# A second tap of VectorE's 3x3 convolution made by ScalarE and added by an accumulating DMA, with the later parts of that convolution one slot later

## The chip, the cores and the metric

The kernel runs on one core of a Trainium2 chip. The metric is device time in microseconds. Three runs of the kernel before took 6636.07, 6640.18 and 6641.82 us (median 6640.18). One more execution was taken with a profile.

## The reference, cut to what matters

The input is x of shape (8, 32, 128, 128), float32: eight images of 32 channels. For the normalised image, block matching picks for each pixel the 8 best of 25 shifts, and the shifted copies are stacked to 256 channels (xb). Then three pairs of a 1x1 convolution and a depthwise 3x3 convolution follow:

```
h = relu(conv(conv(xb, w1), w2, groups=CK, pad=1))
h = relu(conv(conv(h, w3), w4, groups=CK, pad=1))
wiener = sigmoid(conv(conv(h, w5), w6, groups=CK, pad=1))
filt = conv(wiener * dct, inv_dct_w, groups=C)
return conv(filt, agg_w)          # added to x; then a norm and a 5x5 convolution
```

A depthwise 3x3 convolution is, for each channel, a sum of nine shifted copies ("taps") of its image, each multiplied by a weight. All sums are in float32.

## The kernel before, in words

An image is cut into strips of eight rows; a step handles one strip, and there are 17 steps for each of the eight images, 136 in all. Each step has four slots, in the order i = 3, 2, 1, 0. Slot i = 1, 2 or 3 runs convolution pair i ("stage i") on a strip that is older the higher i is; slot 0 multiplies by the dct (`final_dct`, L795 on) and later sums up (`final_add`, L819 on). The strip that stage i began in its slot is read by stage i+1 in the next step, three slots later, and stage 3's by slot 0 of the same step, also three slots later.

The 256 channels are two halves of 128. One half's 3x3 convolution runs on TensorE (`pointwise_t`, `depthwise_t`: matmuls of L694 into p, copy to t at L701, shifted copies t<-t by DMA, matmuls of L750 into pw, activation at L763). The other half's runs on VectorE (`pointwise_v`, `depthwise_v`): the 1x1 result pv (L670) is copied by ScalarE to tv (L678); ScalarE makes the first tap into acc (L721); VectorE adds eight more with scalar_tensor_tensor (L724), in place; ScalarE applies relu or sigmoid (L728); a DMA moves the last two rows of tv to its top for the next strip (`rows_before_v`, L655).

`depthwise_v` is a generator, and the loop over the slots calls its parts. For a stage that begins in slot k: the ScalarE tap is written in slot k, the eight VectorE taps later in slot k, the activation in slot k+1, the row copy in slot k+2. The variables `new_v`, `dv` and `kept` hold the generators of this slot, the last one and the one before that. Slot 0 begins no stage, so it has an empty generator. Inside a slot the order is:

```
pointwise_v; first tap (ScalarE)       # pv, tv, L721
next(later); run("P"); final_dct       # pa (slot 3) ; L809, L817 (slot 0)
run("Q"); gather_select (0,)           # pd ; sel on ScalarE
gather_load; tick(b, i)                # ib ; other work on VectorE
next(later); next(new_v)               # xr, L838 ; VectorE taps, L724
pointwise_t; next(kept)                # p, t ; L655
gather_pixels; next(dt); run("A")      # pg, xb L638 ; pw L750 ; squares L452
next(dv); gather_select (1,); next(dt) # L728 ; sel ; L763
```

The order on TensorE, VectorE and ScalarE is this program order (`manual_schedule`). TensorE, VectorE, ScalarE, POOL (GpSimd) and SP (SyncE) each work their own instructions one after the other; POOL's and SP's are nearly all DMA issues.

Three other things go on beside the stages. The gather: matmuls pg (L631) on selection masks (sel, two ScalarE instructions each, L616 and L617), copied to xb (L638). The block matching of the next image: differences on VectorE (df, L444), squares on ScalarE (L452), matmuls pd (L459), then costs, maxima and places. And the last layer of the image before. Their work is handed out by `tick`, which gives VectorE 0.4 of a step's share in slot 0 and 0.2 in each of slots 3, 2 and 1. Once per image, `sources` writes the next image in another layout (xl, L411, then 32 transfers xtd<-xl in a row, L424 and L429, all from POOL's queue).

PSUM results of many kinds share five buffers in turn (pool `ps_x`): among them pv, p, pg, pa and pc. Each acc tile has one buffer per stage and half.

Of the kernel before, what the change touches and what calls it, by code (L numbers as in the profile page):

```python
# [8 lines left out]
F32 = mybir.dt.float32  # L9
# [3 lines left out]
AF = mybir.ActivationFunctionType  # L13
ALU = mybir.AluOpType
ORDERED = {mybir.EngineType.PE, mybir.EngineType.DVE, mybir.EngineType.Activation}

P = 128
C, K, H, W = 32, 8, 128, 128
CK = C * K
NO = 25  # L20
R = 8
# [23 lines left out]
def bm3d_conv_preact(  # L45
# [16 lines left out]
    nc = tc.nc  # L62
# [60 lines left out]
    dwv = const.tile([P, 3, 9], F32, name="dwv")  # L123
    for n, w in enumerate((w2, w4, w6)):
# [22 lines left out]
        op0=ALU.mult,  # L147
        op1=ALU.add,
# [38 lines left out]
    accp = ctx.enter_context(tc.tile_pool(name="acc", bufs=1))  # L187
# [23 lines left out]
    def push(task):  # L211
        want = next(task, None)
        if want:
            which, cost, *wait = want
            queues[which].append((cost, task, now[0] + (wait[0] if wait else 0)))
# [132 lines left out]
    def bands():  # L348

        nc.sync.dma_start(kb, k5.rearrange("a b -> (a b)").partition_broadcast(P))  # L350
        for dx in range(5):
            yield "D", 1.8
            nc.vector.tensor_scalar(
                band[:, dx], cst[:, 0:P], kb[:, dx : dx + 1], None, op0=ALU.mult
            )
            for i in range(1, 5):
                nc.vector.scalar_tensor_tensor(
                    band[:, dx],
                    cst[:, i : i + P],
                    kb[:, 5 * i + dx : 5 * i + dx + 1],  # L360
                    band[:, dx],
                    op0=ALU.mult,
                    op1=ALU.add,
                )

    def prep(b):

        xn = load_image(b, nc.gpsimd) if b else first
        yield "P", 0
        yield "D", 5.5  # L370
        st = work.tile([P, 8, 6], F32, name=f"st_{b}", tag="st")
        for i in range(8):
            nc.vector.bn_stats(
                st[:, i], xn[:, 3 + 4 * i : 7 + 4 * i, 2 : 2 + W]
            )
        mv = work.tile([P, 2], F32, name=f"mv_{b}", tag="mv")
        nc.vector.bn_aggr(mv, st.rearrange("p a b -> p (a b)"))
        yield "A", 0
        nc.scalar.copy(xn[:, :, 0:2], xn[:, :, 2:3].to_broadcast([P, HR, 2]))
        nc.scalar.copy(  # L380
            xn[:, :, 2 + W :], xn[:, :, 1 + W : 2 + W].to_broadcast([P, HR, 2])
        )
        mr = yield from group_stats(mv, f"a{b}")
        nc.vector.tensor_scalar(
            xn, xn, mr[:, 0:1], mr[:, 1:2], op0=ALU.subtract, op1=ALU.mult
        )
        push(sources(b, xn))

        idx = work.tile([P, 4, 8, K, 4], U32, name=f"idx_{b}", tag="idx", bufs=1)

        sq = dram.tile([NO // 2, 4, HR - 2, HX], F32, name=f"sq_{b}", tag="sq")
        for i in range((HR - 2) // SR):
            pd = ps_d.tile([P, SR // 2, HX], F32, name=f"pd_{b}_{i}", tag="pd")

            for aa in ((2, 4), (0, 0), (1, 1), (3, 2), (4, 3), (5, 5)):
                yield "D", PAIR
                push(squares(b, i, pd, xn, aa, sq, idx))
# [254 lines left out]
    def rows_before_v(i, b, n):  # L652
        v = tv[i - 1]
        if n < NS:
            nc.sync.dma_start(v[:, 0:2], v[:, R : R + 2])  # L655
        else:
            nc.gpsimd.memset(v[:, 0 : i + 1], 0.0)
# [52 lines left out]
    def depthwise_v(i, b, n):  # L710
        v = tv[i - 1]
        nr = R if n < NS else i
        out_ = accp.tile([P, R, W], F32, name=f"acc{i}_{b}_{n}_1", tag=f"acc{i}1")
        acc = out_[:, :nr]
        for k, (dy, dx) in enumerate(
            ((1, 1), (0, 0), (0, 1), (0, 2), (1, 0), (1, 2), (2, 0), (2, 1), (2, 2))
        ):
            tap = dwv[:, i - 1, 3 * dy + dx : 3 * dy + dx + 1]
            rows = v[:, dy : dy + nr, dx : dx + W]
            if k == 0:  # L720
                nc.scalar.activation(acc, rows, AF.Copy, scale=tap)  # L721
                yield out_
            else:
                nc.vector.scalar_tensor_tensor(  # L724
                    acc, rows, tap, acc, op0=ALU.mult, op1=ALU.add
                )
        yield
        nc.scalar.activation(acc, acc, funcs[i - 1])  # L728
        yield
        rows_before_v(i, b, n)  # L730
# [266 lines left out]
    def unit(stage, u, *rest):  # L997
        if 0 <= u < len(units) and units[u]:
            if stage is gather_load:
                at = (units[u][0], units[u][1] % 8 // 2)  # L1000
                until(lambda: at in ready, 4.0)
            stage(*units[u], *rest)
# [20 lines left out]
    def turn(credit):  # L1023
        now[0] += 1
        run("D", credit)
        run("A")
        run("P")
        run("Q")

    def until(cond, credit):  # L1030
        while not cond():
            turn(credit)

    with tc.manual_schedule(engines=ORDERED):
        push(prep(0))
        push(weights())
        push(mixes())
        xbd[0] = dram.tile([P, 2, H, W], F32, name="xbd_0", tag="xbd")
        for i in range(3):
            nc.gpsimd.memset(tb[i][0:64, :, 0], 0.0)  # L1040
        for u in range(7):
            unit(gather_load, u)

            for _ in range({2: 3, 3: 1}.get(u, 0)):
                turn(4.0)
            unit(gather_select, u - 2)
            unit(gather_pixels, u - 3)
        u = 4

        dt = dv = kept = iter(())  # L1050

        later = iter(())

        for s in range(len(steps) + 2):
            if s < len(steps):
                b, n = steps[s]
                if s == 2:
                    push(bands())
                if n == (0 if b else 4) and b + 1 < NB:
                    until(lambda: b in ready, 4.0)  # L1060
                    push(prep(b + 1))
                if n == NS - 1 and b + 1 < NB:
                    until(lambda: b + 1 in ready, 4.0)
                    xbd[b + 1] = dram.tile([P, 2, H, W], F32, name=f"xbd_{b+1}", tag="xbd")
            for i in (3, 2, 1, 0):
                si = s - (i - 1 if i else 2)
                live = 0 <= si < len(steps)
                new_v = new_t = iter(())
                if live:
                    bi, ni = steps[si]  # L1070

                if live and i:
                    src = source(i, bi, ni)
                    pointwise_v(i, bi, ni, lws[i - 1], src)
                    new_v, new_t = depthwise_v(i, bi, ni), depthwise_t(i, bi, ni)
                    accs[i, bi, ni] = [None, next(new_v)]
                next(later, None)
                if live and not i:
                    if ni == 0:
                        x1d[bi] = dram.tile([C, H, W], F32, name=f"x1d_{bi}", tag="x1d")  # L1080
                        stats[bi] = work.tile([P, NS + 1, 6], F32, name=f"stat_{bi}", tag="stat")
                    xr, xf, j0, j1 = fins.pop(si)
                run("P")
                if live and not i:
                    final_dct(bi, ni, accs[3, bi, ni], xf, j0, j1)

                run("Q")
                if s < len(steps):
                    unit(gather_select, u + 1, (0,))
                    unit(gather_load, u + 3)  # L1090
                    tick(b, i)
                next(later, None)
                next(new_v, None)
                if live and i:
                    pointwise_t(i, bi, ni, lws[i - 1], src)
                next(kept, None)
                if s < len(steps):
                    unit(gather_pixels, u)
                next(dt, None)
                run("A")  # L1100
                next(dv, None)
                if s < len(steps):
                    unit(gather_select, u + 1, (1,))
                    u += 1
                next(dt, None)
                kept, dv, dt = dv, new_v, new_t
                if live and not i:
                    later = end(bi, ni, xr, j0, j1)
                if not i and 0 <= s - 1 < len(steps):
                    fins[s - 1] = final_load(*steps[s - 1])  # L1110
        next(kept, None)
        for _ in later:
            pass
        until(lambda: {(NB - 1, 0), (NB - 1, 1)} <= done, 4.0)
# [62 lines left out]
```

## Time and profile before

| | |
|---|---|
| profiled execution, its own time | 6645.45 us |
| its span, first to last instruction | 6643.7 us |
| median of three runs | 6640.18 us |
| mean granted TensorE clock | 0.978 |
| TensorE busy | 6238.3 us, 94% |
| VectorE busy | 5862.9 us, 88% |
| ScalarE busy | 5054.4 us, 76% |
| POOL busy | 3079.3 us, 46% |
| data moved by DMA | 886.20 MB |

Busy is time with an instruction at work; the rest of the span an engine waits. A line of a group reads: line, engine, operation, result<-inputs, shape, xcount, then busy time in us, mean ns of one, and the idle time before them with what ended it. A line of the waits reads: engine, its tile and line, "<-" what it waited for, then total us, times, longest us. PE is TensorE, DVE is VectorE, ACT is ScalarE. A timeline line reads: start us, duration us, engine, line, operation, result<-inputs, shape, xcount. A line of the DMA issues ends with the size of one in KB and the median us from issue to landing.

### The profile page before, as it was taken

What the parts mean: (1) busy time and instruction counts of PE and PEld (TensorE: products, weight loads), DVE (VectorE), ACT (ScalarE), POOL (GpSimd) and SP (SyncE); (2) the same over time, 40 slices, a digit from 0 to 9 for tenths busy, and PEclk for the clock granted to TensorE, in tenths of its full rate; (3) what the DMA queues carried; (4) which work ended last, traced back from release to release, by engine and by line L of the source; (5) the groups of instructions that cost most, each with busy time, mean ns of one, the idle gap of its engine ahead of it and who ended that gap; (6) DMA issues with size and microseconds to landing.
All of it is one profiled execution on the core that took longest, in us unless ns stands there. A gap on an engine that the chain in (4) does not pass through costs nothing.

```text
span 6643.7 us, 234197 instructions
## 1 busy us (share of the span) xinstructions
PE 6238.3 (94%) x102306; PEld 3236.5 (49%) x102306; DVE 5862.9 (88%) x8828; ACT 5054.4 (76%) x6698; POOL 3079.3 (46%) x5015
## 2 busy tenths in 40 slices
PE   5898899999999999999999999999999999999997
PEld 1444455544555545544555544554445544454553
DVE  7889988999889998898989998899888999887786
ACT  5787778777787777877778877887769777687772
POOL 8354346444464343643446444464435543344334
PEclk8899999999999999999999999999999999999998
DMA  4555555656555564655646656465555655556553
GB/s 85 126 138 130 131 131 130 148 134 140 131 143 136 130 147 118 149 134 133 144 121 147 147 126 149 120 154 136 130 137 132 148 136 130 125 141 145 137 133 82
DMA packets 770751, 886.20 MB, mean 133 GB/s; under 512 B 248880, under 2 KB 614000, under 8 KB 769728
## 3 DMA queue, kind: packets, MB, share of 16 engines
q0 software_dynamic: 383648, 611.87, 36.9%
q1 hardware_dynamic: 383568, 258.11, 17.6%
q8 instruction: 805, 13.19, 0.9%
q10 hardware_dynamic: 2512, 1.25, 0.1%
q14 instruction: 218, 1.79, 0.1%
HBM read 420.60 MB, written 216.49 MB: 96 GB/s over the span
## 4 chain that ended last, share of the span: by engine, by line
PE 43%; DVE 29%; DMA 9%; ACT 8%; POOL 6%; issue 4%; SPq 0%; ACTq 0%; DVEq 0%; POOLq 0%
DVE acc L724 20%; PE pw L750 14%; PE pv L670 11%; PE p L694 9%; PE pg L631 3%; DMA t<-t 3%; POOL xtd L424 2%; DVE df L444 2%; DVE idx L537 2%; PE pc L809 2%; ACT sel L616 2%; ACT df L452 2%; DMA xf<-xbd 2%; DVE acc L817 1%; PE p L923 1%
## 5 line engine op out<-in xcount | busy, mean ns | idle before, releaser
L724 DVE SCALAR_TENSOR_TENSOR acc<-tv,dwv,acc 128x1024 f32<-128x1024 f32 (+3 forms) x3264 | 4032.3, 1237 | 240.8 <-ACT acc L721 136.8
L750 PE MATMUL pw<-t,dwd 96*32 96x254 f32 (+7 forms) x31680 | 2124.6, 420 | 51.0 <-DMA t<-t 38.4
L750 PEld LDWEIGHTS pw<-t,dwd 96*32 96x32 f32 (+1 forms) x31680 | 1088.4, 110 | 874.5 <-issue 411.2
L616 ACT ACTIVATE sel<-ib,nplace 128x1024 f32<-128x1024 uint8 x1024 | 1172.1, 1145 | 37.4 <-DMA ib<-idxd 37.4
L617 ACT ACTIVATE sel<-sel 128x1024 f32<-128x1024 f32 x1024 | 1085.7, 1060 | 32.5
L694 PE MATMUL p<-acc,lw 128*32 128x256 f32 x16768 | 1002.9, 383 | 24.7 <-ACT tv L678 23.3
L670 PE MATMUL pv<-acc,lw 128*32 128x512 f32 x8448 | 956.2, 590 | 48.7 <-DVE acc L817 43.4
L602 POOL DMA_DIRECT2D ib<-idxd x512 | 292.5, 571 | 1241.8 <-ACT sel L616 1176.2
L790 POOL DMA_DIRECT2D xf<-xbd x1088 | 651.9, 631 | 316.1 <-PE pc L809 180.1
L694 PEld LDWEIGHTS p<-acc,lw 128*32 128x32 f32 x16768 | 579.2, 111 | 437.1 <-issue 79.4
L452 ACT ACTIVATE df<-df 128x786 f32<-128x786 f32 (+2 forms) x576 | 468.6, 861 | 340.5 <-DVE df L444 337.8
L631 PE MATMUL pg<-sel,xt 120*32 120x88 f32 (+1 forms) x24576 | 616.1, 244 | 63.6 <-ACT sel L617 50.7
L631 PEld LDWEIGHTS pg<-sel,xt 120*32 120x32 f32 x24576 | 556.8, 110 | 235.0 <-ACT sel L617 70.1
L678 ACT COPY tv<-pv 128x512 f32<-128x512 f32 (+2 forms) x784 | 437.1, 579 | 305.0 <-PE pv L670 293.0
L444 DVE TENSOR_TENSOR df<-xn 128x786 f32<-128x786 f32 (+2 forms) x576 | 531.6, 973 | 81.2 <-PE pd L459 80.2
L728 ACT ACTIVATE acc<-acc 128x1024 f32<-128x1024 f32 (+3 forms) x408 | 417.3, 1023 | 241.6 <-DVE acc L724 241.3
L763 ACT ACTIVATE acc<-pw 128x512 f32<-128x512 f32 (+2 forms) x808 | 438.5, 573 | 182.7 <-PE pw L750 182.0
L670 PEld LDWEIGHTS pv<-acc,lw 128*32 128x32 f32 x8448 | 286.0, 111 | 534.1 <-issue 428.7
L701 ACT COPY t<-p 128x512 f32<-128x512 f32 x800 | 424.4, 571 | 118.0 <-PE p L694 118.0
L721 ACT ACTIVATE acc<-tv,dwv 128x1024 f32<-128x1024 f32 (+3 forms) x408 | 454.9, 1115 | 33.9 <-PE pa L830 20.6
L670 PE MATMUL pv<-xb,lw 128*32 128x512 f32 x4096 | 473.5, 596 | 0.0
L694 PE MATMUL p<-xb,lw 128*32 128x256 f32 x8192 | 468.5, 379 | 1.0 <-DVE xy L935 0.9
(155 smaller groups left out, 5932.9 us busy)
## 6 DMA issues: line engine op xcount, KB each, us to landing
ib<-idxd POOLq DMA_DIRECT2D x512, 256.0 KB, 4.1
xbd<-xb POOLq DMA_DIRECT2D x128, 1024.0 KB, 5.9
xf<-xbd POOLq DMA_DIRECT2D x960, 128.0 KB, 7.1
t<-t SPq DMA_DIRECT2D x792, 128.0 KB
t<-t SPq DMA_DIRECT2D x384, 256.0 KB
tv<-tv SPq DMA_DIRECT2D x384, 130.0 KB
xt<-xtd POOLq DMA_DIRECT2D x240, 180.0 KB, 3.7
xtd<-xl POOLq DMA_DIRECT2D x192, 96.0 KB, 3.5
```

What stands on the lines that cost most here:

```text
L444: nc.vector.tensor_sub(df[:, :, ca:cz], xn[:, r0 : r0 + SR, ca:cz], xn[:, r0 + dy : r0 + dy + SR, ca + dx : cz + dx],)
L452: nc.scalar.activation(df[:, :, ca:cz], df[:, :, ca:cz], AF.Square)
L616: nc.scalar.activation(sel, ib, AF.Square, bias=nplace)
L617: nc.scalar.activation(sel, sel, AF.Relu, scale=-1.0, bias=1.0)
L631: nc.tensor.matmul(pg[C * j : C * (j + 1), :, :, xa:xz], xt[: 8 * QW, f * (NT // 2) + t], sels[j // 2][: 8 * QW, j % 2 * 2 : j % 2 * 2 + 2 ...
L670: nc.tensor.matmul(ps[C * j : C * (j + 1), :hr], lhsT[:, g, P + C * j : P + C * (j + 1)], src(g)[:, h : h + hr], start=g == 0, stop=g == 1,)
L694: nc.tensor.matmul(ps[C * r : C * (r + 1), e, :nb], lhsT[:, g, s], rows[:, r : r + 4 * nb - 3 : 4], start=g == 0, stop=g == 1,)
L721: nc.scalar.activation(acc, rows, AF.Copy, scale=tap)
L724: nc.vector.scalar_tensor_tensor(acc, rows, tap, acc, op0=ALU.mult, op1=ALU.add)
L750: nc.tensor.matmul(pt[u][C * j : C * (j + 1), ka:kz, :nb, xa:xz], dwd[0:hi, i - 1, u, j, dx + 1], t[0:hi, j, ka:kz, :nb, xa + dx : xz + dx ...
L763: nc.scalar.activation(rows[:, u : u + 2 * nh[u] - 1 : 2, :nb], pt[u][:, : nh[u], :nb], funcs[i - 1])
L790: nc.gpsimd.dma_start(xf[p : p + C, m, j0:j1], src[g, m, (h + m + 1) % 2, :, :, ya:yz])
```

## The change

In `depthwise_v` ScalarE makes two taps: (1, 1) into acc as before, and (0, 0) into a new tile "more" with one buffer. A DMA from POOL's queue adds "more" to acc (`accum_op=ALU.add`). VectorE adds the other seven taps. The taps of VectorE now come after the first yield, and the loop calls them in slot k+1, the activation in slot k+2 and the row copy in slot k+3; `dv1`, `dv2` and `dv3` hold the generators of the last three slots. The places inside a slot where taps, activation and row copy are called stay the same, and so does `tick`.

```
+        more = accp.tile([P, R, W], F32, name=f"more{i}_{b}_{n}", tag="more")[:, :nr]
         acc = out_[:, :nr]
-        for k, (dy, dx) in enumerate(
-            ((1, 1), (0, 0), (0, 1), (0, 2), (1, 0), (1, 2), (2, 0), (2, 1), (2, 2))
-        ):
-            tap = dwv[:, i - 1, 3 * dy + dx : 3 * dy + dx + 1]
+        def tap(dy, dx):
             rows = v[:, dy : dy + nr, dx : dx + W]
-            if k == 0:
-                nc.scalar.activation(acc, rows, AF.Copy, scale=tap)
-                yield out_
-            else:
-                nc.vector.scalar_tensor_tensor(
-                    acc, rows, tap, acc, op0=ALU.mult, op1=ALU.add
-                )
+            return rows, dwv[:, i - 1, 3 * dy + dx : 3 * dy + dx + 1]
+        for to, at in ((acc, (1, 1)), (more, (0, 0))):
+            rows, scale = tap(*at)
+            nc.scalar.activation(to, rows, AF.Copy, scale=scale)
+        nc.gpsimd.dma_start(acc, more, accum_op=ALU.add)
+        yield out_
+        for at in ((0, 1), (0, 2), (1, 0), (1, 2), (2, 0), (2, 1), (2, 2)):
+            rows, scale = tap(*at)
+            nc.vector.scalar_tensor_tensor(
+                acc, rows, scale, acc, op0=ALU.mult, op1=ALU.add
+            )
         yield
         nc.scalar.activation(acc, acc, funcs[i - 1])
...
-                next(new_v, None)
+                next(dv1, None)
...
-                next(kept, None)
+                next(dv3, None)
...
-                next(dv, None)
+                next(dv2, None)
...
-                kept, dv, dt = dv, new_v, new_t
+                dv3, dv2, dv1, dt = dv2, dv1, new_v, new_t
```

## The prediction

> **What bounds the kernel now.** I read the page's busy shares first, then TensorE's waits, then the three engines' timelines around one boundary between slots. The page:
>
> ```profile
> PE 6238.3 (94%) x102306; PEld 3236.5 (49%) x102306; DVE 5862.9 (88%) x8828; ACT 5054.4 (76%) x6698; POOL 3079.3 (46%) x5015
> ...
> PE 43%; DVE 29%; DMA 9%; ACT 8%; POOL 6%; issue 4%; SPq 0%; ACTq 0%; DVEq 0%; POOLq 0%
> ...
> L724 DVE SCALAR_TENSOR_TENSOR acc<-tv,dwv,acc 128x1024 f32<-128x1024 f32 (+3 forms) x3264 | 4032.3, 1237 | 240.8 <-ACT acc L721 136.8
> ```
>
> The 94% is real work: 96 matmuls of L750 take 5.3 us wherever I look, in crowded stretches and in quiet ones, so nothing is stretched. The view by windows gives PE 5941 us busy in the 6200 us between 200 and 6400. Its idle time there is 259 us, 1.9 us for each of the 136 steps (8 images x 17). That is all that relief on another engine can give back. TensorE's waits (total us, times, longest) say who could:
>
> ```profile
> PE pi L569 <- DVE oc L560: 63.2, 16, 20.2
> PE pg L631 <- ACT sel L617: 50.7, 33, 2.3
> PE pd L459 <- ACT df L452: 46.6, 47, 3.6
> PE pv L670 <- DVE acc L817: 43.4, 25, 3.0
> PE pw L750 <- DMA t<-t: 38.4, 27, 4.0
> ```
>
> The first, third and fourth come from a late VectorE (df is made there). VectorE's 29% of the chain is mostly where it runs beside a TensorE that is busy anyway. So the change relieves the second engine, and what matters is whether it adds a wait to the first.
>
> **What goes and comes.** 408 taps leave VectorE: 408 x 1.237 = 505 us (5863 to 5358). 408 taps come to ScalarE: the present L721 tap takes 1.115 us in the mean, so +455 us (5054 to 5509). 408 accumulating transfers, up to 512 KB each, come to POOL's queue: at 0.5 to 0.8 us an issue (rows xf 0.63, xl 0.76) 200 to 330 us more of POOL's 46%.
>
> **What moves.** Taps, activation and row copy of the VectorE half each run one slot later than now. A step has slots 3, 2, 1, 0; stage i+1 consumes stage i three slots after it began. Now the activation L728 lies in the second slot, a whole slot ahead of its reader. After the change it lies at the end of the third, and the reader opens the next slot. What stands between them, stage by stage:
> - Stage 3: L728 at the end of slot 1; its reader is VectorE's L817 in slot 0. TensorE's pw (5.3) and pc (1.9) lie between: free.
> - Stage 2: L728 in slot 0; pw (5.3 us) lies between it and stage 3's pv. ScalarE needs the xb copy 0.6, perhaps squares 1.7, L728 1.06: covered.
> - Stage 1: L728 falls in slot 3, which has no pw, as slot 0 begins no stage. TensorE goes from pg straight to stage 2's pv (slot 2). Nothing lies between.
>
> TensorE and then ScalarE at that last boundary, now (start, duration, instruction; a step with squares):
>
> ```profile
> 4511.22 1.06 PE L830 MATMUL pa<-acc,lagg 128*32 128x256 f32 x16
> 4512.08 0.86 PE L459 MATMUL pd<-df,neg 128*32 128x396 f32 x8
> 4512.75 3.65 PE L694 MATMUL p<-acc,lw 128*32 128x256 f32 x64
> 4516.20 1.14 PE L631 MATMUL pg<-sel,xt 120*32 120x88 f32 x48
> 4517.15 3.62 PE L670 MATMUL pv<-acc,lw 128*32 128x512 f32 x32
> ```
> ```profile
> 4512.39 1.15 ACT L721 ACTIVATE acc<-tv,dwv 128x1024 f32<-128x1024 f32 x1 [0.34 <-PE pa L830]
> ...
> 4517.40 0.59 ACT L638 COPY xb<-pg 128x512 f32<-128x512 f32 x1 [0.36 <-PE pg L631]
> 4517.88 1.61 ACT L452 ACTIVATE df<-df 128x786 f32<-128x786 f32 x2
> 4519.39 1.14 ACT L616 ACTIVATE sel<-ib,nplace 128x1024 f32<-128x1024 uint8 x1
> ```
>
> ScalarE runs in program order, and the code puts L728 between the squares (L452) and that sel (L616). It can't start before the xb copy, which needs the pg that ends as pv begins. pv reads the half that L728 writes from its fifth matmul on, 0.43 us in.
>
> **Term 1, the new wait of pv.** ScalarE's path: the xb copy ends 0.84 us after pv's start (also the median over the 134 boundaries that I read in the timelines), L728 takes 1.06 to 1.1, less 0.43: 1.5 us a step, 201 us in all; squares ahead of it make it 3.1. VectorE's path: L817 ends 1.4 us after pc where it isn't late, then follow the work of two ticks (mean 5.6 us, up to 10), then seven taps (7 x 1.315 = 9.2), then L728: 17.3 us after pc's end, against 17.5 + 0.43 that TensorE takes from there. So it is even in the mean and late by some us where ticks are heavy: slot 0 keeps its double share (0.4) of the other work and now gets stage 1's taps too. Step by step, the later of both paths gives 2.2 us a step (298) if L817 is always on time, 2.7 (358) if it is at most 3 us late, and 4.1 (550) with today's lateness (mean 5.6). Bounds 201 and 550. I take 358, since VectorE sheds 1.3 us a slot and no longer waits for a tap of the same slot, yet gets its work bunched.
>
> **Term 2, POOL's queue.** The transfer must be issued and landed before the next slot's second tap rewrites "more" (one buffer) and before VectorE's taps. Slot 3 to slot 2 above: two taps end at 4514.7, the next slot's second would start at 4523.7, so 9.0 us; less an issue of 0.7, the landing may take 8.3. Nearest rows:
>
> ```profile
> xbd<-xb POOLq DMA_DIRECT2D x128, 1024.0 KB, 5.9
> xf<-xbd POOLq DMA_DIRECT2D x960, 128.0 KB, 7.1
> ```
>
> It fits in most slots. It doesn't behind this, once per image:
>
> ```profile
> 4350.97 24.63 POOL L424 DMA_DIRECT2D xtd<-xl  x30
> 4375.59 1.47 POOL L429 DMA_DIRECT2D xtd<-xl  x2
> ```
>
> A transfer that becomes ready a slot (12 us) after this run begins waits 26.1 - 12 = 14 us, less some 5 of slack: 9 us, for seven images 60. Bounds 0 and 7 x 26 = 180. The Trainium skill, "DMA: Bandwidth & Descriptors", section "SWDGE vs HWDGE vs iDMA", says that accumulating is to be had only from GpSimd's queue. That speaks against the change: SP's quieter queue is no way out. No row shows an accumulating transfer from either; were SP open to it, this term would be 0 and the sum 6870. The same page, "Anatomy of one DMA", fits 2.0 us + bytes/436e3, an estimate of 3.2 us for 512 KB, which would leave 5 us to spare; but it makes 2.3 us of the 128 KB for which the row has 7.1, so the rows decide.
>
> **Terms at nothing.** ScalarE's 455 us: its waits for TensorE (tv 293, L763 182, xb 152, t 118: 745 us) cover them; without that cover sel comes late for pg, 0 to 150. The DMA engines: 55% busy now; 214 MB more on 886, twice if reading the destination counts, delays t<-t ahead of pw: 0 to 100, hidden in slot 2 by the pv wait itself. Rows of tv copied a slot later: VectorE's taps are equally far behind as now, so 0.
>
> **Term 3, what comes back.** The waits on a late VectorE (63 + 43 + 47 us and smaller ones) mostly go, and each stall lets the others catch up: -130, bounds 0 and -259. After them the next late thing is term 1 itself.
>
> **Sum.** 358 + 60 - 130 = +288 us on the profiled 6645.45 us (6643.7 span and 1.75 around it): 6933. The median of the runs shown is 5 below: 6930 us, +4.4%. Without trouble on the way, 201 - 130 is +71; all upper ends but for term 3's half: 550 + 180 + 150 + 100 - 130 = +850, too pessimistic, as one wait hides another.
>
> **Rivals.**
> - Faster. VectorE was the true drag: the chain gives it 29%. TensorE's stall is the floor of 1.5 us and nearly all idle time comes back: 201 - 259 = -58, 6580 us; it decides if more than the floor's 1.5 of the 1.9 us idle per step returns. Against it: waits on sel, t<-t and tv (112 us of the rows) have nothing to do with VectorE's taps. 0.12.
> - Much slower, transfer-bound. If landing takes over 8.3 us as a rule (xf's 128 KB has 7.1, out's 124 KB 11), ScalarE waits for "more" in two or three slots a step: at 1 us in each of some 300 of the 408 slots +300 on top of the 288, 7230 us. 0.14.
> - Nothing that can be told: stall and return cancel within 0.2% (about what a measurement of this kernel can tell from no change). 0.04.
> - Forecast: 0.70, alone 6720 to 7150 (+71 above, and 550 + 60 - 100).
>
> The range 6660 to 7300 reaches from 201 less 190 returned to a little beyond the transfer-bound case; it leaves out the faster rival and the far tail. Faster 0.12, same 0.04, slower 0.84.
>
> **What would show it.** In the changed profile: TensorE's wait "pv <- ACT acc (L728's line)" in the hundreds of us, nearly all in slot 2, each 1.5 us or more, where there is none now; VectorE near 5360 busy and with more idle time; ScalarE near 5510; the waits pi <- oc and pv <- L817 shrunk; some ScalarE or VectorE waits on a DMA of acc<-more just behind the xtd run. I am wrong if pv doesn't wait for that activation, if TensorE's idle time stays under 405 us, or if the taps wait for the transfer all the time.

## The result and the profile after

The changed kernel takes 7173.36 us (median of four runs, 7153.98 to 7176.58), beside 6641.0 us for the kernel before: 1.0793 times as long, 95% interval 1.0773 to 1.0814. The profiled execution spans 7174.8 us. The forecast was 6930 with a range to 7300.

First the busy shares and three groups of the page after (in the changed file VectorE's taps are L728, ScalarE's two L723, the accumulating transfer L724, the activation L732; L670 is still pv):

```profile
PE 6382.0 (89%) x102306; PEld 3231.6 (45%) x102306; DVE 5359.8 (75%) x8420; ACT 5470.6 (76%) x7106; POOL 3444.3 (48%) x5423
...
L728 DVE SCALAR_TENSOR_TENSOR acc<-tv,dwv,acc 128x1024 f32<-128x1024 f32 (+2 forms) x2856 | 3531.4, 1237 | 950.5 <-DMA acc<-more 611.1
...
L670 PE MATMUL pv<-acc,lw 128*32 128x512 f32 x8448 | 1082.0, 638 | 334.5 <-ACT acc L732 331.6
...
L723 ACT ACTIVATE more<-tv,dwv 128x1024 f32<-128x1024 f32 (+3 forms) x408 | 448.9, 1100 | 292.6 <-DMA acc<-more 292.6
```

VectorE lost its 503 us as meant, and TensorE pays. TensorE's idle time (span less busy) went from 405 to 793 us, and its busy time from 6238 to 6382 for the same 102306 matmuls. 388 + 144 = 532 us, all of the loss. TensorE's waits now begin with one that was not there:

```profile
PE pv L670 <- ACT acc L732: 331.6, 170, 5.5
PE pg L631 <- ACT sel L617: 74.5, 35, 4.3
PE pw L754 <- DMA t<-t: 66.7, 32, 5.7
```

This is how one looks in the timelines of TensorE and of ScalarE, at the boundary from slot 3 to slot 2 that the prediction had drawn:

```profile
4704.13 1.13 PE L631 MATMUL pg<-sel,xt 120*32 120x88 f32 x48
4705.07 1.04 PE L670 MATMUL pv<-acc,lw 128*32 128x512 f32 x8
4710.42 4.11 PE L670 MATMUL pv<-acc,lw 128*32 128x512 f32 x24 [4.31 <-ACT acc L732]
```
```profile
4705.82 0.60 ACT L638 COPY xb<-pg 128x512 f32<-128x512 f32 x1
4706.30 3.13 ACT L452 ACTIVATE df<-df 128x792 f32<-128x792 f32 x4
4709.31 1.06 ACT L732 ACTIVATE acc<-acc 128x1024 f32<-128x1024 f32 x1
```

pv stops after its first matmuls (the profile shows eight before the gap) until ScalarE has done the copy of pg, the squares and the activation, in that order. But the 24 matmuls behind the gap take 4.11 us, where 32 take 3.6 elsewhere. The view by windows shows why (columns: stretch, length, busy time of PE, PEld, DVE, ACT and POOL, then the granted clock, the DMA share and GB/s):

```profile
4705.00:4710.00 5.00, 1.11 (x24) 0.20 (x12) 4.86 (x7) 5.00 (x8) 5.00 (x8) 0.97 0.77 182
4710.00:4714.00 4.00, 3.58 (x24) 0.91 (x24) 1.35 (x2) 2.98 (x4) 4.00 (x5) 0.61 0.65 146
4714.00:4718.00 4.00, 4.00 (x62) 1.93 (x58) 0.00 (x0) 1.74 (x2) 4.00 (x6) 1.00 0.48 112
```

The granted clock falls to 0.61 for the 4 us after the gap. That accounts for the growth of TensorE's busy time: the trace's clock records give half speed for 699 us of the span, where it was 290 us before. Weighed with the time in which TensorE was busy, that is a loss of 164 us more than before, an estimate from those records, beside the 144 us of growth. The mean clock of the whole execution is 0.951, where it was 0.978.

The other new waits are VectorE's and ScalarE's for the transfer, from their lists of waits:

```profile
DVE acc L728 <- DMA acc<-more: 611.1, 84, 20.8
DVE acc L821 <- PE pc L813: 336.0, 101, 12.6
DVE acc L728 <- issue: 199.7, 15, 20.8
```
```profile
ACT more L723 <- DMA acc<-more: 292.6, 39, 16.1
```

The longest are of 20 us, several times the median landing of 5.5 us in the list of DMA issues. POOL's timeline shows where they come from. At 4692.79 the run of xtd transfers begins, and a transfer whose second tap was ready soon after stands behind all of it:

```profile
4692.79 24.61 POOL L424 DMA_DIRECT2D xtd<-xl  x30 [1.14 <-DMA xl<-xs]
4717.39 1.47 POOL L429 DMA_DIRECT2D xtd<-xl  x2
4718.85 4.49 POOL L794 DMA_DIRECT2D xf<-xbd  x8
4723.33 0.97 POOL L724 DMA_DIRECT2D acc<-more  x1
```

ScalarE's second tap of that transfer ended at 4702.4. ScalarE itself then idles 14.2 us before its next "more", as there is one buffer.

### The profile page after: what moved, and what is told of

It is laid out like the page before. It is cut to its first block, busy times and chain, and to the rows that moved or that the text cites. A ratio compares the mean times of both kernels' runs of the same rounds, so it can differ in the third digit from the quotient of the medians.

```text
span 7174.8 us, 234926 instructions
## 1 busy us (share of the span) xinstructions
PE 6382.0 (89%) x102306; PEld 3231.6 (45%) x102306; DVE 5359.8 (75%) x8420; ACT 5470.6 (76%) x7106; POOL 3444.3 (48%) x5423
## 5 line engine op out<-in xcount | busy, mean ns | idle before, releaser
L728 DVE SCALAR_TENSOR_TENSOR acc<-tv,dwv,acc 128x1024 f32<-128x1024 f32 (+2 forms) x2856 | 3531.4, 1237 | 950.5 <-DMA acc<-more 611.1
L754 PE MATMUL pw<-t,dwd 96*32 96x254 f32 (+7 forms) x31680 | 2160.0, 426 | 83.1 <-DMA t<-t 66.7
L754 PEld LDWEIGHTS pw<-t,dwd 96*32 96x32 f32 (+1 forms) x31680 | 1104.6, 112 | 933.9 <-issue 415.6
L670 PE MATMUL pv<-acc,lw 128*32 128x512 f32 x8448 | 1082.0, 638 | 334.5 <-ACT acc L732 331.6
L724 POOL DMA_DIRECT2D acc<-more x408 | 379.8, 931 | 1351.0 <-ACT more L723 1035.3
L694 PE MATMUL p<-acc,lw 128*32 128x256 f32 x16768 | 984.8, 382 | 40.3 <-DVE xy L939 40.3
L694 PEld LDWEIGHTS p<-acc,lw 128*32 128x32 f32 x16768 | 564.6, 111 | 462.2 <-issue 94.2
L670 PEld LDWEIGHTS pv<-acc,lw 128*32 128x32 f32 x8448 | 281.7, 117 | 923.3 <-ACT acc L732 491.3
L723 ACT ACTIVATE more<-tv,dwv 128x1024 f32<-128x1024 f32 (+3 forms) x408 | 448.9, 1100 | 292.6 <-DMA acc<-more 292.6
L767 ACT ACTIVATE acc<-pw 128x512 f32<-128x512 f32 (+2 forms) x808 | 441.6, 574 | 281.8 <-PE pw L754 279.8
L602 POOL DMA_DIRECT2D ib<-idxd x512 | 338.5, 664 | 635.3 <-ACT sel L616 597.3
L821 DVE TENSOR_TENSOR acc<-acc,pc 128x512 f32<-128x512 f32 (+1 forms) x528 | 321.0, 665 | 356.1 <-PE pc L813 336.0
L670 PE MATMUL pv<-xb,lw 128*32 128x512 f32 x4096 | 476.1, 604 | 28.0 <-ACT bc L868 28.0
```

What stands on the lines that cost most here:

```text
L670: nc.tensor.matmul(ps[C * j : C * (j + 1), :hr], lhsT[:, g, P + C * j : P + C * (j + 1)], src(g)[:, h : h + hr], start=g == 0, stop=g == 1,)
L694: nc.tensor.matmul(ps[C * r : C * (r + 1), e, :nb], lhsT[:, g, s], rows[:, r : r + 4 * nb - 3 : 4], start=g == 0, stop=g == 1,)
L723: nc.scalar.activation(to, rows, AF.Copy, scale=scale)
L728: nc.vector.scalar_tensor_tensor(acc, rows, scale, acc, op0=ALU.mult, op1=ALU.add)
L754: nc.tensor.matmul(pt[u][C * j : C * (j + 1), ka:kz, :nb, xa:xz], dwd[0:hi, i - 1, u, j, dx + 1], t[0:hi, j, ka:kz, :nb, xa + dx : xz + dx ...
```

## Experiments

The theory was that the shift of the activation (a new wait of pv) is the larger part of the loss and a late transfer the smaller. The rival was that the transfer is the whole. Each number is the median less that of the kernel before measured beside it (6641 to 6654 us).

**Relief alone.** The kernel before with one tap dropped from VectorE's list:

```
-            ((1, 1), (0, 0), (0, 1), (0, 2), ...
+            ((1, 1), (0, 1), (0, 2), ...
```

> The kernel before with VectorE's tap (0,0) left out (it is not added anywhere), nothing moved: VectorE loses 505 us, nobody gets anything. It measures what relief of VectorE is worth by itself. Theory (TensorE bounds, relief gives back the waits on a late VectorE): 6510 us, between 6380 (all of the 259 us of idle TensorE between 200 and 6400) and 6600. Rival (VectorE was never on the path): within 0.5% of 6641.

Measured: 6490.87 us, -156, ratio 0.9774 (0.9754 to 0.9794). VectorE's relief has a worth by itself, about what the prediction's third term said, and not its 505 us. TensorE's span less busy is 297 us here, where it was 405; its busy time fell as well, from 6238.3 to 6177.0 us.

**Shift and relief.** The changed kernel without second tap and transfer:

```
-        more = accp.tile(...)
-        for to, at in ((acc, (1, 1)), (more, (0, 0))):
+        for to, at in ((acc, (1, 1)),):
-        nc.gpsimd.dma_start(acc, more, accum_op=ALU.add)
```

> The changed kernel without the second ScalarE tap and without the accumulating transfer: tap (0,0) is left out of the sum, VectorE makes seven taps one slot later, all later parts as in the change. Theory A (the price is the slot shift: stage 2's pv waits for stage 1's activation): the wait pv <- ACT acc stays at 300 us or more, TensorE's clock drops behind the long ones, and the time stays at 6850 to 7000. Theory B (the price is the transfer): the time falls to about that of the relief alone, 6500 to 6650.

Measured: 6797.72 us, +151, ratio 1.0227 (1.0210 to 1.0244). That is 52 us under theory A's span and 148 above B's. The wait of pv is there with no transfer in the kernel at all: 260.3 us, 155 times, a little under the 300 that A had said. Against the relief alone, the shift costs 307 us.

**With ScalarE's tap.** Only the transfer is left out:

```
-        nc.gpsimd.dma_start(acc, more, accum_op=ALU.add)
```

> The changed kernel without the accumulating transfer alone: ScalarE still makes the second tap into its own tile, which is not added, so tap (0,0) is left out of the sum. Against the run without that tap it prices ScalarE's 455 us. Theory A: 20 to 100 us more than that run, since ScalarE's tap lies ahead of the activation that pv waits for. Theory B: no more than 20 us. The distance from here to the changed kernel's 7173 is the transfer's own price: A says 150 to 300, B 400 or more.

Measured: 6866.08 us, +219, ratio 1.0329 (1.0312 to 1.0346). ScalarE's second tap adds 363 us to its busy time (5110.4 to 5473.0) and costs 68. The rest to the changed kernel, 313 us, is the transfer's. So neither theory holds as put: shift and transfer are alike in size, and A's upper bound of 300 for the transfer was a little low.

**Three buffers.** The second tap goes to the buffer of the same stage's TensorE half, which is idle then:

```
-        more = accp.tile([P, R, W], F32, name=..., tag="more")
+        more = accp.tile([P, R, W], F32, name=..., tag=f"acc{i}0")
```

> The changed kernel, whole, with the second tap in the buffer of the same stage's other half (one per stage, three in all) in place of one shared buffer. ScalarE's wait for a landing (293 us in the changed kernel) must go. Theory A (ScalarE held by the shared buffer passes its stall on to TensorE): 7173 less 150 to 250, 6920 to 7020. Theory B (the same transfer is late for VectorE's taps just as well, 611 us of waits there): within 50 us of 7173.

Measured: 7122.42 us, +476, ratio 1.0712 (1.0694 to 1.0729), 57 us better than the changed kernel. Theory B was nearly right: ScalarE's wait of 293 us is gone (72 us of waits for a landing are new, in front of the other half's activation), but VectorE's idle time before the first of its taps, whatever ended it, is 805 us, where it was 861. So freeing ScalarE gave back little, as VectorE waits for the same transfers.

**Traffic only.** As the last, but the transfer adds into a tile that nobody reads:

```
-        nc.gpsimd.dma_start(acc, more, accum_op=ALU.add)
+        nc.gpsimd.dma_start(spare[:, :nr], more, accum_op=ALU.add)
```

> The changed kernel with three buffers for the second tap, but the transfer adds it into a spare tile that nobody reads: tap (0,0) is left out of the sum. The same 512 KB move at the same place of POOL's queue, and VectorE's taps wait for no transfer. Theory A (the transfer costs what it does by being late for VectorE, from POOL's queue): 6866 (no transfer) to 6940. Theory B (the traffic slows the other transfers, t<-t above all): 7020 to 7120, and the wait pw <- t<-t stays at 60 us or more.

Measured: 6935.93 us, +293, ratio 1.0447 (1.0430 to 1.0464), theory A's upper end. Moving the bytes (and issuing them) costs 74 us, in which 81 us of ScalarE's waits for a landing may have a part, as the second tap's buffer is the one that the other half's activation writes; that VectorE must wait for them costs 183 more. The wait pw <- t<-t is 40 us here.

**POOL's queue cleared.** The changed kernel with:

```
         for j in range(QW):
+            if b:
+                yield "P", 0
...
-                yield "A", 0, 1
+                yield "A", 0, 3
                 load(c + 8)
```

> The changed kernel, whole, with POOL's queue less blocked: the xtd run is issued two transfers per slot instead of 32 in a row, and the last layer's reload of xy comes two slots later, when the stores it waits for have landed. Theory A (transfers are late because they stand behind these in POOL's order): VectorE's waits for the transfer fall from 800 to 500 us or less, the time by 60 to 180, to 6990 to 7110. Theory B (landing and traffic): within 30 us of 7173.

Measured: 7107.19 us, +464, ratio 1.0693 (1.0669 to 1.0718): 68 us better, at A's low end. VectorE's waits for the transfer fell from 611 to 460 us, but the wait remains. Over the 408 transfers of the changed kernel, I set VectorE's idle time before the first tap against the time from the end of the second ScalarE tap to POOL's issue: 36 transfers issued over 3 us late carry 509 us, and only seven of these stood behind xtd (132 us). Another 24 (334 us) stood behind the last layer's stores. For twelve of them it is as below: POOL waits for VectorE's xy, the four issues take 6 us, and then POOL waits until stores have landed before it reloads xy. The other twelve stood behind loads of xf that waited for stores to land in the same way.

```profile
3206.98 6.08 POOL L941 DMA_DIRECT2D out_dram<-xy  x4 [6.88 <-DVE xy L939]
3220.41 0.79 POOL L888 DMA_DIRECT2D xy<-x1d  x1 [7.35 <-PE pv L670]
3221.19 0.95 POOL L724 DMA_DIRECT2D acc<-more  x1
```

The label in the second line names pv, but two of the four stores had landed at 3217.18 and 3219.83, and the issue came 0.58 us after the second.

Another 74 transfers issued in time still had VectorE idle over 1 us, 343 us in all. Each of these waits ended as the transfer landed, and in 38 of them VectorE had come even before the issue. With the queue cleared, late transfers carry 235 us (23 of them) in place of 509, and those issued in time 337: so 275 us less of VectorE's late waits gave back 68 us, and the waits for a landing stayed.

**Activation early.** The run without the transfer, with one call moved:

```
                 next(dv3, None)
+                next(dv2, None)
                 if s < len(steps):
                     unit(gather_pixels, u)
                 next(dt, None)
                 run("A")
-                next(dv2, None)
```

> The run without the transfer (tap (0,0) left out of the sum), with one call moved: the activation is issued ahead of the gather's copy and the squares of its slot, not behind them. Theory A (pv waits because the activation stands behind the xb copy and the squares on ScalarE): the wait pv <- ACT acc falls from 313 us to under 120, the time from 6866 to 6600 to 6720. Theory B (VectorE's bunched taps in slot 0 make the activation late): the wait passes to ACT acc <- DVE acc and the time stays above 6800.

Measured: 6677.07 us, +34, ratio 1.0047 (1.0030 to 1.0064). One moved line gives back 185 us of the shift's 307, with the same work on every engine. Without and with the move, TensorE's longest wait reads:

```profile
PE pv L670 <- ACT acc L731: 313.2, 160, 5.5
```
```profile
PE pv L670 <- ACT acc L731: 129.6, 127, 6.0
```

So pv waited because the activation stood behind the xb copy and the squares, as theory A had it, though its wait stayed a little over the 120 us that A had said. VectorE's bunched taps are not what is left either: ScalarE's wait "acc <- DVE acc" is 21.4 us in this run. What is left of the shift, 140 us between this run and the run "ScalarE's tap, unshifted" below, was not taken apart further.

**All mended.** The changed kernel with three buffers, early activation, cleared POOL queue, and:

```
-        ... * (0.4 if i == 0 else 0.2)
+        ... * (0.4 if i == 3 else 0.2)
```

> The changed kernel, whole, with three buffers, the earlier activation, the cleared POOL queue, and the double share of other VectorE work moved from slot 0 to slot 3, which has no taps now. Theory A: savings add up, 7173 less 50, 150 to 250, 60 to 180 and some 30: 6650 to 6900, not under the kernel before, since ScalarE's 455 us and the landing stay. Theory B (relief of VectorE is worth it once the waits are mended): under 6641.

Measured: 6834.77 us, +192, ratio 1.0282 (1.0263 to 1.0300). The savings add up about as said, and it stays slower than the kernel before. TensorE's first wait is now pw <- t<-t, 172.0 us, up to 15.9 at once. SP, which issues t<-t, waits 1911 us for VectorE's taps before the row copies of tv, so a late VectorE could hold up t<-t too. But that wait is 2019 us in the changed kernel, where pw <- t<-t is 66.7 us; what made the 172 us stays open.

**The add behind the taps.** No shift. ScalarE's two taps and VectorE's seven stay in one slot, POOL adds after them, and the activation comes two slots after the taps, early in its slot:

```
         for at in ((0, 1), ..., (2, 2)):
             nc.vector.scalar_tensor_tensor(acc, rows, scale, acc, ...)
+        nc.gpsimd.dma_start(acc, more, accum_op=ALU.add)
...
                     accs[i, bi, ni] = [None, next(new_v)]
+                next(kept, None)
...
-                next(dv, None)
```

> A whole kernel without the slot shift: ScalarE's two taps and VectorE's seven in the same slot as before, the transfer adds the second tap behind VectorE's taps, and the activation two slots after the taps, early in its slot. Nobody on VectorE waits for the transfer, and stage 2's pv has a full ScalarE stretch between it and the activation. From the runs so far: 6491 for the relief, +68 for ScalarE's tap, +70 for the traffic: 6629, between 6590 and 6700, so at best a little under the kernel before. Rival (the transfer, now waiting for VectorE at POOL, holds up POOL's other transfers): over 6700 with VectorE or TensorE waiting for POOL's loads.

Measured: 6838.05 us, +184, ratio 1.0292 (1.0270 to 1.0314). A miss. The second tap's buffer is the one that L767, the other half's activation, writes a slot later, and ScalarE now waits there for the landing: 501.5 us.

**ScalarE's tap, unshifted.** The kernel before with that tap made but not added:

> The kernel before with tap (0,0) made by ScalarE into its own tile, which is not added (tap (0,0) left out of the sum), nothing moved. Against the relief alone (6491) it prices ScalarE's 455 us where no slot is shifted: theory A 30 to 80 us more, as in the shifted pair (+68); rival (there ScalarE's tap cost only because it lay ahead of the activation that pv waits for): within 20 us of 6491.

Measured: 6548.25 us, -106, ratio 0.9848 (0.9830 to 0.9867). The tap costs 50 us here, 68 in the shifted pair, which the intervals can hardly tell apart. So most of it is ScalarE's load by itself.

**The add behind the taps, xtd spread.**

> The run with the add behind the taps, whole, and the xtd run issued two transfers per slot for all images but the first. Theory: 0 to 60 us less than without the spread, as the add no longer stands behind 26 us of issues; no change if nothing waits for it there.

Measured: 6734.86 us, +81, ratio 1.0124 (1.0106 to 1.0142). 103 us better, more than expected. What remains is led by ScalarE's wait in front of the other half's activation:

```profile
ACT acc L769 <- DMA acc<-more: 527.5, 131, 18.3
```

**Own buffers.** The last run with the second tap made behind the copies to t, in buffers that the other half's activation doesn't write:

```
+        tag = "more" if i != 2 else "acc10"
...
         yield
+        more = accp.tile([P, R, W], F32, name=..., tag=tag)[:, :nr]
+        rows, scale = tap(0, 0)
+        nc.scalar.activation(more, rows, AF.Copy, scale=scale)
         nc.gpsimd.dma_start(acc, more, accum_op=ALU.add)
...
                     pointwise_t(i, bi, ni, lws[i - 1], src)
+                next(new_v, None)
```

> The run with the add behind the taps and the spread xtd run (6735), whole, with the second ScalarE tap made later in its slot, behind the copies to t, and kept in buffers that the TensorE half's activation doesn't need (one shared by stages 3 and 1, stage 2's in stage 1's idle one). The activation's wait for a landing, 527 us there, must go. Theory (what is left above 6548 is 70 us of traffic and this wait): 6580 to 6650, so level with the kernel before or a little under it. Rival (the traffic and POOL's blocked queue are what is left): 6690 or more.

Measured: 6631.07 us, -17, ratio 0.9976 (0.9961 to 0.9991). That wait is gone, and ScalarE's for a landing is 86.6 us, now before the acc activation. The idea of the change can be made to pay, by a quarter of a per cent; the interval lies just under 1.

The ladder, from the kernel before to the changed one:

| step | us |
|---|---|
| VectorE relieved of a tap | -156 |
| taps, activation and row copy a slot later | +307 |
| ScalarE makes the tap | +68 |
| the transfer moves its bytes | +74 |
| VectorE waits for it | +183 |
| one buffer for all second taps | +57 |
| sum (measured: +532) | +533 |

The price of a step depends on what stands below it; this is the order in which I took them off. By the intervals, each is uncertain by some 15 to 20 us.

## Why the prediction was right or wrong

The direction, the mechanism of the first term and the range held. The size was about half (288 of 532 us): the sum was 358 + 60 + 0 + 0 - 130, and in the same terms the runs gave 307 + 240 + 68 + 74 - 156.

- **What bounds the kernel.** Right in the main. The 532 us are TensorE's idle and slowed time, and 492 us less on VectorE (the run with relief alone) brought 156. But "nothing is stretched" was too much said: that relief took 61 us off TensorE's busy time as well, so idle time was not all that could come back.
- **Term 1, pv's wait, 358 (201 to 550).** Right in place and cause, near in size: 307 as an experiment, with a direct wait of 260 us in that run. In the changed kernel 279 of the 332 us fall at the boundary from slot 3 to slot 2, as said; 53 us fall at stage 3's pv, which was called covered. That the size is near is in part luck, as the mixture was off. VectorE's late taps hardly count (ScalarE's wait "acc <- DVE acc" is 13.5 us after the change, 241.3 before), ScalarE's path is the later one, and part of the price is the clock behind the gaps, which I had not counted: with the shift, TensorE's busy time is 86 us longer (6177.0 to 6262.5). And the floor of 1.5 us was misread. The profile has 32 records for pv's 16 matmuls, so the half that the activation writes is needed from the ninth record on, 1.04 us in (the eight records before the gap above) and not 0.43; that makes the floor 0.9 us, and the commonest gap with the shift alone is 0.8 us (62 of 172).
- **Term 2, POOL's queue, 60 (0 to 180).** This is the term that failed, by its size: waiting for the transfer and its one buffer cost 240 us (183 + 57 in the ladder), over the upper bound. I took xtd for the only run that could make it late. The last layer's stores, with POOL waiting behind them for their landing, make more late than xtd does (334 us of VectorE's waits, against 132). And I gave 5 us of slack, for which no row stands: 8.3 less the landings of 5.9 and 7.1 leaves 1 to 2.5 us, and VectorE, once relieved, came to 74 transfers that were issued in time before they had landed (343 us).
- **Terms at nothing.** ScalarE's tap was put at 0 (0 to 150), and cost 50 to 68: "its waits for TensorE cover them" held for a part of it only (the four waits named shrank from 837 to 594 us as the tap came to the relieved kernel). Which of ScalarE's later instructions then came late was not tried. The DMA engines' load was put at 0 (0 to 100); traffic and issue cost 74.
- **Term 3, what comes back, -130.** Right: -156 in the run with relief alone. Of the waits named, pi <- oc fell from 63.2 to 39.2, and pv <- L817 left the list.
- **The transfer-bound rival.** Its 7230 lies nearer to the result than my 6930, but its condition didn't hold: the median landing is 5.5 us, under its 8.3. Late issues carry 509 us of VectorE's waits and landings of usual length 343 us; how the 183 us of TensorE's time split between them is open, as clearing the queue gave back 68 us only. The faster rival fell with the shift: relief reaches 6491 only where nothing else is changed.
- **The fit of "DMA: Bandwidth & Descriptors", section "Anatomy of one DMA".** The estimate from it was 3.2 us for 512 KB; the accumulating transfers land in 5.5 us in the median. The measurement decides; of the 5 us to spare it leaves 2.8. Whether another engine's queue could accumulate was not tried.

## What to carry to other kernels

Before moving a step to a later slot, look up for each stage what the bounding engine does between the moved step and its reader, and what stands ahead of that step on its own engine; here one slot of three had nothing between, and one call moved four lines up gave back 185 us. A transfer in place of an instruction is as late as the queue that it stands in, so count that queue's longest runs and its waits for landings, and ask whether the reader comes before a landing of usual length. And ask first what relief is worth by itself: dropping the work in one run said 156 us for 492 us of VectorE's time, which left little for the price of the means.

## What the hardware showed that I had not expected

**The clock behind a gap.** Where TensorE idled 0.5 to 1.8 us before pv's remaining matmuls (88 times in the changed kernel), the next 23 started over 2.19 us, but for two cases of 4.0 to 4.1. Behind gaps of 2.2 to 3 us (25 times, 20 of them slowed) they took 1.17 us more in the mean, behind 3 to 6 us (30 times) 1.68 us more. The Trainium skill, "TensorE: Matmul & The Clock Gate", section "Part 1: The HAM clock gate (the "warmup" mystery)", has the clock halved after an idle window of about 3.4 us; here gaps well under that were often enough. So a stall of 2.5 us cost about 3.7 in the mean, an estimate from these figures.

**Accumulating transfers.** POOL needs 0.93 us to issue one, where most others take 0.5 to 0.8. From the queues' shares (36.9% of 6643.7 us before, 50.0% of 7174.8 after) one can estimate that 408 of them kept the 16 DMA engines busy for 1136 us more, 2.8 us each for up to 512 KB.

**POOL's issue can wait for a landing.** After the last layer's stores POOL stood still until some had landed before it issued xf, though xf needs nothing of them: 92.1 us in 42 waits in the changed kernel, and 83.3 us in 49 before. The trace shows what held it. The transfers of this queue use eight semaphores in turn, and in the changed kernel none of the 5222 issues came before the transfer eight places before it had landed. In all 42 waits that transfer was a store, and xf was issued 0.3 to 0.8 us after its landing. So it is the way in which this program reuses its semaphores, and a store that takes 11.3 us to land blocks what comes eight issues later.
